# A pause on GpSimd that waits for SyncE's answer, and one-hots made by a scalar for each edge

## The chip, the cores and the metric

The kernel runs on one core of one Trainium2 chip. The metric is the device time of one execution in microseconds (us); lower is better. The engines are named as the profile names them: PE is TensorE, DVE is VectorE, ACT is ScalarE, POOL is GpSimd and SP is SyncE, which here only issues DMAs and waits.

## The reference, cut to what matters

A graph network of three layers over 6250 nodes with 256 features and 100000 edges, sorted by the node that they end in:

```python
ew = edge_attr @ edge_w + edge_b                       # 100000 x 256, the same in each layer
for l in range(3):
    residual = x
    msg = relu(x[src] * ew)                            # the gather of 100000 rows
    for i in range(3):                                 # by edge type
        h = segment_sum(msg * (edge_type == i), dst)   # 6250 x 256
        out += (h / max(count_i, 1)) @ weights[l, i]
    out += x @ roots[l] + biases[l]
    x = residual + relu(out)
return layernorm(x0 + x)
```

## The kernel before, in words

The edges are cut into 391 pairs; a pair is 2 x 128 edges, and two pairs share one row buffer (a quad, `xs`, 128 x 2 x 2 x 256). The 391 pairs of a layer are walked in one hand-written order, one loop step `it` for each; a step takes up several pairs at different stages:

- `gather` (nine pairs ahead): `gather_pair` issues two indirect DMAs from POOL's queue (L900), each of which fetches 128 rows of 1 KB by the indices in `src_i`, and behind them zeroes a tile `breath` of 128 x 256 that nothing reads (L904). The first six pairs of a layer are gathered in the layer before (`gather_early`). Eight quads of row buffers rotate.
- `make_ew` (PE, L602 and L606): the weights of the edges, into PSUM.
- `weigh` (about three pairs ahead): DVE multiplies the gathered rows by them (L627), ACT takes the relu (L629).
- `one_hot` (two pairs ahead, once for a quad): DVE compares the numbers 0 to 119 with the place of each edge, for four columns of 128 edges at once (L634, 128 x 480). In layer 0 it also adds the two one-hots of a pair into one bf16 tile (L638), for counting.
- `reduce` (PE, L644): four fp32 matmuls sum the pair's rows by the one-hots into `h_p`; in layer 0 a bf16 matmul against ones counts the edges (L647).
- `add` (DVE, L659): adds `h_p` into an accumulator `acc`, at a place read from a register.

Every few pairs a block of 128 nodes is finished (`node_mul`, `node_end`): PE multiplies `acc` by the layer's weights (L687), DVE scales and adds (L718, L721), and SP writes the block to `x_mid` (L723), from which the next layer gathers. In the last layer the block is normalised instead (L738) and written out (L740). SP also loads the edge attributes (`load_at`, L560), 147 times in all, and the weights.

Each engine works through its instructions in the order in which they are written here (`tc.manual_schedule()`); waits between engines are put in from the tiles that they share. At the start of layer 0, twelve comparisons with a scalar for each partition (`find_came`, L568) stand in DVE's order.

Of the kernel before, what the change touches and what calls it, by code (L numbers as in the profile page):

```python
# [8 lines left out]
F32 = mybir.dt.float32  # L9
BF = mybir.dt.bfloat16  # L10
I32 = mybir.dt.int32
AF = mybir.ActivationFunctionType
ALU = mybir.AluOpType
# [429 lines left out]
def ordered_path(ctx, tc, x, attr_laid, A, weights, roots, biases, edge_w, edge_b, out, src, src_i, seg, place_i, consts, x_root,  # L443
# [6 lines left out]
    nc = tc.nc  # L450
    P = 128
# [8 lines left out]
    DC = D // P  # L460
    WK = R * WIN
# [10 lines left out]
    ident, ones, iota_w = consts  # L472
# [3 lines left out]
    x_mid = [dram.tile([N, D], F32, name=f"x_mid{l}") for l in range(L - 1)]  # L476

    big = ctx.enter_context(tc.tile_pool(name="big", bufs=1))
# [26 lines left out]

    acc = big.tile([P, DC + 1, R, ASIDE + 2 * P + WIN], F32, name="acc")
    inv = big.tile([P, NT, R], F32, name="inv")
    breath = big.tile([P, 256], F32, name="breath")
    zero = big.tile([P, 1], F32, name="zero_o")
    nc.vector.memset(zero, 0.0)  # L510
    eps = big.tile([P, 1], F32, name="eps")
# [1 line left out]
    full_ones = big.tile([P, P], BF, name="full_ones")  # L513
# [15 lines left out]
    edge = ctx.enter_context(tc.tile_pool(name="edge", bufs=2))  # L529
# [7 lines left out]
    def first_of(p, n):  # L537
        return p == 0 or order[p - 1] // n != order[p] // n
# [31 lines left out]
    def layer(l, r_sb, b_sb, ats, early, pools):  # L570
# [5 lines left out]
        x_rows = x if l == 0 else x_mid[l - 1]  # L576
        w_sb = wpool.tile([P, R * DC, D], F32, name="w_sb")
        CH = DC + 1 if l == 0 else DC
        xs, ew_ps, ohs, h_ps, o_ps, rs = {}, {}, {}, {}, {}, {}
        x0s, mvs, oh_bs, t_ss, places = {}, {}, {}, {}, []  # L580
        r_next, ats_next, early_next = (None, None), {}, {}

        def gather(u):
            p = order.index(u)
            if p < FIRST:
                xs[u // 2] = early[u // 2]
            else:
                if first_of(p, 2):
                    xs[u // 2] = room(rows, D)
                gather_pair(nc, xs[u // 2], x_rows, src_i, u, breath)  # L590

        def pairs_of(q):
            return range(min(2, U - 2 * q))
# [15 lines left out]
        def gather_early(p):  # L609
            u = order[p]  # L610
            if first_of(p, 2):
                early_next[u // 2] = room(rows, D)
            gather_pair(nc, early_next[u // 2], x_mid[l], src_i, u, breath)

        def complete(q):
            for k in pairs_of(q):
# [14 lines left out]
        def one_hot(q):  # L631
            ohs[q] = edge.tile([P, 4, WK], F32, name="oh", bufs=3)
            n = 2 * len(pairs_of(q))
            nc.vector.tensor_tensor(ohs[q][:, :n, :], iota_w[:, None, :].to_broadcast([P, n, WK]),  # L634
                                    seg[:, 4 * q:4 * q + n, None].to_broadcast([P, n, WK]), op=ALU.is_equal)
            if l == 0:
                oh_bs[q] = edge.tile([P, 2, WK], BF, name="oh_b", bufs=3)
                nc.vector.tensor_tensor(oh_bs[q][:, :n // 2], ohs[q][:, 0:n:2], ohs[q][:, 1:n:2], op=ALU.add)  # L638

        def reduce(u):  # L640
            h_ps[u] = h_pool.tile([P, DC + 1, WK], F32, name="h_p")
            for d in range(DC):
                for i in range(2):
                    nc.tensor.matmul(h_ps[u][:, d, :], xs[u // 2][:, u % 2, i, d * P:(d + 1) * P],  # L644
                                     ohs[u // 2][:, u % 2 * 2 + i, :], start=(i == 0), stop=(i == 1))
            if l == 0:
                nc.tensor.matmul(h_ps[u][:, DC, :], full_ones, oh_bs[u // 2][:, u % 2, :], start=True, stop=True)  # L647

        def add(u):
            if places[:1] != [u // 8]:  # L650
# [109 lines left out]
        for it in range(-11, max(starts) + 7):  # L760
            def pair(k):
                return order[it + k] if 0 <= it + k < U else None
            if pair(AHEAD) is not None:
                gather(pair(AHEAD))
            if l < L - 1 and 0 <= it + AHEAD - U < FIRST:
                gather_early(it + AHEAD - U)
# [15 lines left out]
            if pair(0) is not None:  # L782
                reduce(pair(0))
# [39 lines left out]
            if pair(2) is not None and first_of(it + 2, 2):  # L823
                one_hot(pair(2) // 2)
# [68 lines left out]
def room(rows, D):  # L893

    return rows.tile([128, 2, 2, D], F32, name="xs", bufs=ROWS)


def gather_pair(nc, xs, x_rows, src_i, u, breath=None):
    for i in range(2):
        nc.gpsimd.indirect_dma_start(  # L900
            out=xs[:, u % 2, i, :], out_offset=None, in_=x_rows[:, :],
            in_offset=bass.IndirectOffsetOnAxis(ap=src_i[:, 2 * u + i:2 * u + i + 1], axis=0))
    if breath is not None:
        nc.gpsimd.memset(breath, 0.0)  # L904


@with_exitstack
def kernel(ctx, tc, x, src, dst, edge_attr, edge_type, weights, roots, biases, edge_w,
# [32 lines left out]
    with tc.tile_pool(name="look", bufs=1) as look, tc.tile_pool(name="look_p", bufs=2, space=PSUM) as look_p, \  # L941
# [17 lines left out]
        for u in schedule(N, E, 1)[0][:FIRST]:  # L959
            if u // 2 not in first_rows:  # L960
                j = 4 * len(first_rows)
                first_rows[u // 2] = x_root[:, j:j + 4, :].rearrange("p (k i) d -> p k i d", k=2)
            gather_pair(nc, first_rows[u // 2], x, src_i, u)
# [49 lines left out]
    with tc.If(unordered == 0):  # L1013
        ordered_path(tc, x, attr_laid, edge_attr.shape[1], weights, roots, biases, edge_w, edge_b, out, src, src_i, seg, place_i,
                     (ident, ones, iota_w), x_root, first_rows, node_i)
# [51 lines left out]
```

## Time and profile before

| | |
|---|---|
| time, median of 3 runs | 3261.3 us (3259.16 to 3263.47) |
| the profiled execution | 3254.66 us, its span 3252.8 us |
| busy: PE, DVE, ACT, POOL | 2544.4, 2047.7, 816.6, 2671.8 us |
| gathers on POOL (L900) | 2334 after the first 12 |
| zeroings on POOL (L904) | 1167 |
| mean granted clock of PE | 0.893 |

The span is the profiled execution as the engines saw it; its own time is 1.9 us longer. [...] "Issue" as a cause of idle time means that nothing that the profile shows was waited for.

### The profile page before, as it was taken

How to read it: one execution, taken by the hardware profiler on the slowest of the kernel's cores; microseconds unless marked ns; L12 is line 12 of the kernel's file. 1: busy time of each engine (PE TensorE's matmuls, PEld its weight loads, DVE VectorE, ACT ScalarE, POOL GpSimd, SP SyncE). 2: the span in 40 equal slices, each digit the busy share in tenths (PEclk: the TensorE clock that was granted, in tenths of full speed). 3: DMA queues.
4: the chain of work that ended last, by engine and by line, in shares of the span. 5: the costliest groups of instructions: out<-in, count | busy, mean ns of one | idle time of the engine just before them, and what ended most of it. 6: DMA issues, size and time to landing. Idle time of an engine off the chain costs nothing.

```text
span 3252.8 us, 53355 instructions
## 1 busy us (share of the span) xinstructions
PE 2544.4 (78%) x18484; PEld 2119.3 (65%) x18484; DVE 2047.7 (63%) x4306; ACT 816.6 (25%) x959; POOL 2671.8 (82%) x3522
## 2 busy tenths in 40 slices
PE   5888787888887778777878778777778777777776
PEld 4766666666666666666666666666666666666655
DVE  7766667777776555555555565455656666766754
ACT  2222222222222222222222222222222222222221
POOL 7888888888888788888888888878888888888886
PEclk9888989999998888889889898788888889999988
DMA  5444444334443334333334444434444444444433
GB/s 174 116 129 124 132 117 116 115 114 118 115 126 114 116 103 117 111 111 115 115 114 118 119 118 120 123 107 131 120 123 123 124 123 126 122 120 117 126 108 89
DMA packets 173312, 387.75 MB, mean 119 GB/s; under 512 B 43418, under 2 KB 78636, under 8 KB 173036
## 3 DMA queue, kind: packets, MB, share of 16 engines
q0 software_dynamic: 112608, 307.65, 33.4%
q1 hardware_dynamic: 53136, 68.50, 6.6%
q10 hardware_dynamic: 7292, 8.11, 0.8%
q8 instruction: 151, 2.47, 0.3%
q14 instruction: 125, 1.02, 0.1%
HBM read 364.62 MB, written 19.46 MB: 118 GB/s over the span
## 4 chain that ended last, share of the span: by engine, by line
POOL 63%; issue 14%; PE 12%; DMA 7%; DVE 3%; ACT 1%; POOLq 1%; DVEq 0%; ACTq 0%
POOL xs L900 54%; POOL breath L904 9%; PE h_p L644 5%; DMA xs<-x_mid,src_io 4%; PE o_p L687 3%; DMA xs<-in_x_dram,src_io 2%; PE ew_p L606 2%; DVE xs L627 1%; PE r_p L672 1%; PE ew_p L602 1%; POOLq L900 1%; DVE acc L659 0%; ACT xs L629 0%; DVE x_root L718 0%; ACT acc L704 0%
## 5 line engine op out<-in xcount | busy, mean ns | idle before, releaser
L900 POOL DMA_INDIRECT xs<-x_mid,src_io x1564 | 1520.1, 972 | 375.0 <-issue 357.9
L644 PE MATMUL h_p<-oh,xs 128*128 128x120 f32 x9336 | 1378.4, 300 | 283.8 <-DVE acc L659 212.1
L644 PEld LDWEIGHTS h_p<-oh,xs 128*128 128x128 f32 x9336 | 1279.8, 211 | 448.8 <-DVE acc L659 275.7
L627 DVE TENSOR_TENSOR xs<-ew_p,xs 128x512 f32<-128x512 f32 x1167 | 788.2, 687 | 998.1 <-DMA xs<-x_mid,src_io 689.4
L629 ACT ACTIVATE xs<-xs 128x1024 f32<-128x1024 f32 (+1 forms) x588 | 617.7, 1051 | 2360.3 <-DVE xs L627 2316.7
L900 POOL DMA_INDIRECT xs<-in_x_dram,src_io x770 | 757.5, 984 | 180.8 <-issue 176.4
L659 DVE TENSOR_TENSOR acc<-h_p,acc 128x240 f32 (+1 forms) x1173 | 519.4, 443 | 84.7 <-PE o_p L687 36.5
L687 PE MATMUL o_p<-w_sb,acc 128*128 128x256 f32 (+1 forms) x1716 | 487.9, 425 | 67.7 <-DVE x_root L718 34.6
L606 PEld LDWEIGHTS ew_p<-ew_sb,at 32*128 32x128 f32 x4692 | 287.8, 214 | 272.3 <-issue 265.3
L687 PEld LDWEIGHTS o_p<-w_sb,acc 128*128 128x128 f32 (+1 forms) x1716 | 340.7, 211 | 150.9 <-DVE acc L659 35.6
L602 PE MATMUL ew_p<-bias,full_ones 3*128 3x512 bf16 x1173 | 219.6, 407 | 270.4 <-DVE xs L627 255.1
L606 PE MATMUL ew_p<-ew_sb,at 32*128 32x256 f32 x4692 | 414.9, 448 | 3.9 <-issue 3.9
L904 POOL MEMSET breath<- 128x256 f32 x1167 | 384.9, 330 | 0.4
L634 DVE TENSOR_TENSOR oh<-iota_w,seg_o 128x480 f32<-128x480 f32 x588 | 381.8, 649 | 0.0
L672 PE MATMUL r_p<-r_sb,t_s 128*128 128x256 f32 x588 | 190.8, 455 | 60.4 <-ACT t_s L668 59.6
L718 DVE SCALAR_TENSOR_TENSOR x_root<-o_p,inv,x_root 128x256 f32<-128x256 f32 (+1 forms) x429 | 205.9, 480 | 32.2 <-PE o_p L687 25.1
L672 PEld LDWEIGHTS r_p<-r_sb,t_s 128*128 128x128 f32 x588 | 121.9, 230 | 82.8 <-ACT t_s L668 67.7
L704 ACT ACTIVATE acc<-zero_o 128x768 f32<-128x768 f32 (+1 forms) x150 | 140.3, 935 | 29.3 <-PE r_p L687 18.7
L602 PEld LDWEIGHTS <-full_ones 3*128 3x128 bf16 x1173 | 34.0, 91 | 120.2 <-issue 87.2
L647 PE MATMUL h_p<-oh_b,full_ones 128*128 128x120 bf16 x391 | 88.0, 225 | 0.0
L638 DVE TENSOR_TENSOR oh_b<-oh 128x240 bf16<-128x240 f32 x196 | 80.6, 411 | 6.7
L675 DVE TENSOR_TENSOR x_root<-r_p,b_sb 128x256 f32<-128x256 f32 x147 | 61.3, 417 | 10.5 <-PE r_p L672 8.9
(93 smaller groups left out, 554.8 us busy)
## 6 DMA issues: line engine op xcount, KB each, us to landing
at<-in_attr_laid_dram SPq DMA_DIRECT2D x147, 256.0 KB
xs<-x_mid,src_io POOLq DMA_INDIRECT x1564
xs<-in_x_dram,src_io POOLq DMA_INDIRECT x770
x_mid<-x_all SPq DMA_DIRECT2D x96, 128.0 KB
x_all<-in_x_dram ACTq DMA_DIRECT2D x8, 768.0 KB
x<-in_x_dram SPq DMA_DIRECT2D x48, 128.0 KB
out_dram<-x_all SPq DMA_DIRECT2D x48, 128.0 KB
w_sb<-in_L_gnn_weights_dram SPq DMA_DIRECT2D x3, 768.0 KB
```

Of the source, the lines that this page charges most:

```text
L602: nc.tensor.matmul(banks[j].rearrange("p i d -> p (i d)"), full_ones[j * A:j * A + PARTS, :], bias[j * A:j * A + PARTS].rearrange("p i d - ...
L606: nc.tensor.matmul(banks[j][:, i, :], ats[OCT * o // GROUP][j * A:(j + 1) * A, o % (GROUP // OCT), i, :], ew_sb[j * A:(j + 1) * A, :], sta ...
L627: nc.vector.tensor_mul(xs[q][:, k], ew_ps[2 * q + k], xs[q][:, k])
L629: nc.scalar.activation(there, there, AF.Relu)
L634: nc.vector.tensor_tensor(ohs[q][:, :n, :], iota_w[:, None, :].to_broadcast([P, n, WK]), seg[:, 4 * q:4 * q + n, None].to_broadcast([P, n, ...
L644: nc.tensor.matmul(h_ps[u][:, d, :], xs[u // 2][:, u % 2, i, d * P:(d + 1) * P], ohs[u // 2][:, u % 2 * 2 + i, :], start=(i == 0), stop=(i ...
L659: nc.vector.tensor_tensor(there, h_ps[u][:, :CH].rearrange("p c (r w) -> p c r w", r=R), there, op=ALU.add)
L672: nc.tensor.matmul(rs[c][:, 1, :], t_ss[c][:, d, :], r_sb[:, d, :], start=(d == 0), stop=(d == DC - 1))
L687: nc.tensor.matmul(o_p[:n, j, :], acc[:, d, r, slot:slot + n], w_sb[:, r * DC + d, :], start=(d == 0), stop=(d == DC - 1))
L718: nc.vector.scalar_tensor_tensor(root, o_p[:n, j, :], inv[:n, c, r:r + 1], root, op0=ALU.mult, op1=ALU.add)
L900: nc.gpsimd.indirect_dma_start(out=xs[:, u % 2, i, :], out_offset=None, in_=x_rows[:, :], in_offset=bass.IndirectOffsetOnAxis(ap=src_i[:, ...
L904: nc.gpsimd.memset(breath, 0.0)
```

## The change

`breath`, a tile of float32, becomes `echo`, of int32 and the same size. Behind each zeroing, SP is told to load a value of it whose bounds are 0 and 0. Since that value is known, the built program has no load: what is left on SP is one instruction that waits for POOL's zeroing and then counts up a semaphore of SP. The next pair's zeroing overwrites what SP would have read, so it waits for that count; on POOL this is an instruction of its own, which stands between the pair's second gather and its zeroing. There are 1167 answers in SP's order, among its 352 DMAs, and each stands where its gather stands in the loop.

The one-hots of a quad are made by four comparisons of 128 x 120, each with one scalar for each partition, in place of one of 128 x 480 between two tensors. In layer 0 the bf16 copy holds all four one-hots, not the two sums, and is made by ACT, not DVE; PE counts with two bf16 matmuls for each pair, not one.

```diff
-    breath = big.tile([P, 256], F32, name="breath")
+    echo = big.tile([P, 256], I32, name="echo")
...
-            nc.vector.tensor_tensor(ohs[q][:, :n, :], iota_w[:, None, :].to_broadcast([P, n, WK]),
-                                    seg[:, 4 * q:4 * q + n, None].to_broadcast([P, n, WK]), op=ALU.is_equal)
+            for t in range(n):
+                nc.vector.tensor_scalar(ohs[q][:, t, :], iota_w, seg[:, 4 * q + t:4 * q + t + 1], None,
+                                        op0=ALU.is_equal)
             if l == 0:
-                oh_bs[q] = edge.tile([P, 2, WK], BF, name="oh_b", bufs=3)
-                nc.vector.tensor_tensor(oh_bs[q][:, :n // 2], ohs[q][:, 0:n:2], ohs[q][:, 1:n:2], op=ALU.add)
+                oh_bs[q] = edge.tile([P, 4, WK], BF, name="oh_b", bufs=3)
+                nc.scalar.activation(oh_bs[q][:, :n], ohs[q][:, :n], AF.Copy)
 
         def reduce(u):
             h_ps[u] = h_pool.tile([P, DC + 1, WK], F32, name="h_p")
-            for d in range(DC):
+            for d in range(CH):
                 for i in range(2):
-                    nc.tensor.matmul(h_ps[u][:, d, :], xs[u // 2][:, u % 2, i, d * P:(d + 1) * P],
-                                     ohs[u // 2][:, u % 2 * 2 + i, :], start=(i == 0), stop=(i == 1))
-            if l == 0:
-                nc.tensor.matmul(h_ps[u][:, DC, :], full_ones, oh_bs[u // 2][:, u % 2, :], start=True, stop=True)
+                    nc.tensor.matmul(h_ps[u][:, d, :],
+                                     xs[u // 2][:, u % 2, i, d * P:(d + 1) * P] if d < DC else full_ones,
+                                     (ohs if d < DC else oh_bs)[u // 2][:, u % 2 * 2 + i, :],
+                                     start=(i == 0), stop=(i == 1))
...
-    if breath is not None:
-        nc.gpsimd.memset(breath, 0.0)
+    if echo is not None:
+        nc.gpsimd.memset(echo, 0)
+        nc.values_load_multi_w_load_instructions(echo[0:1, 0:1], engines=[mybir.EngineType.SP], min_val=0, max_val=0,
+                                                 skip_runtime_bounds_check_because="it is nought")
```

More of the change, by code (lines that the diff above doesn't have):

```diff
@@ L589, in gather @@
                     xs[u // 2] = room(rows, D)
-                gather_pair(nc, xs[u // 2], x_rows, src_i, u, breath)
+                gather_pair(nc, xs[u // 2], x_rows, src_i, u, echo)
         def pairs_of(q):
@@ L612, in gather_early @@
                 early_next[u // 2] = room(rows, D)
-            gather_pair(nc, early_next[u // 2], x_mid[l], src_i, u, breath)
+            gather_pair(nc, early_next[u // 2], x_mid[l], src_i, u, echo)
         def complete(q):
@@ L895, in room, with gather_pair @@
     return rows.tile([128, 2, 2, D], F32, name="xs", bufs=ROWS)
-def gather_pair(nc, xs, x_rows, src_i, u, breath=None):
+def gather_pair(nc, xs, x_rows, src_i, u, echo=None):
     for i in range(2):
```

## The prediction

> **What bounds the kernel now.** I read the page first: busy times, the chain that ended last, the costliest groups.
>
> ```profile
> span 3252.8 us, 53355 instructions
> ...
> PE 2544.4 (78%) x18484; PEld 2119.3 (65%) x18484; DVE 2047.7 (63%) x4306; ACT 816.6 (25%) x959; POOL 2671.8 (82%) x3522
> ...
> POOL 63%; issue 14%; PE 12%; DMA 7%; DVE 3%; ACT 1%; POOLq 1%; DVEq 0%; ACTq 0%
> ...
> L900 POOL DMA_INDIRECT xs<-x_mid,src_io x1564 | 1520.1, 972 | 375.0 <-issue 357.9
> ...
> L627 DVE TENSOR_TENSOR xs<-ew_p,xs 128x512 f32<-128x512 f32 x1167 | 788.2, 687 | 998.1 <-DMA xs<-x_mid,src_io 689.4
> L629 ACT ACTIVATE xs<-xs 128x1024 f32<-128x1024 f32 (+1 forms) x588 | 617.7, 1051 | 2360.3 <-DVE xs L627 2316.7
> L900 POOL DMA_INDIRECT xs<-in_x_dram,src_io x770 | 757.5, 984 | 180.8 <-issue 176.4
> ...
> L904 POOL MEMSET breath<- 128x256 f32 x1167 | 384.9, 330 | 0.4
> L634 DVE TENSOR_TENSOR oh<-iota_w,seg_o 128x480 f32<-128x480 f32 x588 | 381.8, 649 | 0.0
> ...
> L638 DVE TENSOR_TENSOR oh_b<-oh 128x240 bf16<-128x240 f32 x196 | 80.6, 411 | 6.7
> ```
>
> POOL sets the time. Its busy time and the idle time before the gathers, nearly all of it "issue", make 2671.8 + 375.0 + 180.8 = 3227.6 us of a span of 3252.8 us. DVE, by contrast, stands idle for 998.1 us in front of L627, mostly waiting for gathered rows. The timeline of POOL in layer 1 shows the beat:
>
> ```profile
> 1502.42 0.95 POOL L900 DMA_INDIRECT xs<-x_mid,src_io  x1 [0.17 <-issue]
> 1503.68 0.95 POOL L900 DMA_INDIRECT xs<-x_mid,src_io  x1 [0.31 <-issue]
> 1504.63 0.33 POOL L904 MEMSET breath<- 128x256 f32 x1
> 1505.12 0.95 POOL L900 DMA_INDIRECT xs<-x_mid,src_io  x1 [0.17 <-issue]
> ```
>
> A pair costs 1505.12 - 1502.42 = 2.70 us, and 1167 pairs make 3151 us. What changes the time must therefore change this beat: a longer gather, a longer pause, or a gap. So I looked at where the beat is broken.
>
> **Gathers that DVE lengthens.** By line, with shortest, middle and longest duration (ns):
>
> ```profile
> L900 POOL DMA_INDIRECT xs<-x_mid,src_io x1564: 942/952/1738, 1084.7 to 3233.6; - x196
> L900 POOL DMA_INDIRECT xs<-in_x_dram,src_io x770: 942/952/1435, 20.9 to 1083.1; - x193
> L900 POOLq EVENT_SEMAPHORE  x587: 17/43/43, 62.8 to 3226.9; - x196
> L904 POOL MEMSET breath<- x1167: 325/330/457, 23.3 to 3234.6; 128x256 f32 x195
> L904 POOLq EVENT_SEMAPHORE  x2: 43/604/1165, 14.9 to 16.2; - x2
> ```
>
> And from the timeline, a gather that is lengthened and, in the last line, the DVE instruction beside the first gather above:
>
> ```profile
> 1508.85 0.65 DVE L634 TENSOR_TENSOR oh<-iota_w,seg_o 128x480 f32<-128x480 f32 x1
> 1509.07 1.25 POOL L900 DMA_INDIRECT xs<-x_mid,src_io  x1 [0.30 <-issue]
> ...
> 1502.48 0.65 DVE L634 TENSOR_TENSOR oh<-iota_w,seg_o 128x480 f32<-128x480 f32 x1
> ```
>
> The middle gather takes 952 ns, the means are 972 and 984. The surplus is 1564 x 20 + 770 x 32 = 31.3 + 24.6 = 56 us. It comes from the one-hot. L634 at 1508.85, in front of the gather at 1509.07, makes that gather 1.25 us; L634 at 1502.48, just behind the gather at 1502.42, leaves it at 0.95. I matched all gathers in the trace with the DVE instruction running as they start: 244 exceed 948 ns by over 50 ns, 62 us together, and 219 of them (56 us) start inside an L634 or L638. Both read two SBUF tensors. The gather needs something at its start that they hold until they end.
>
> **The one-hots: what goes, what comes.** Both L634 and L638 leave DVE, so up to 56 us of longer gathers go with them: 0.095 us for each of 588 quads. In their place come 588 x 4 less 6 = 2346 comparisons with a scalar for each partition. The nearest row is L568, twelve such comparisons of 128 x 128 in a row:
>
> ```profile
> L956 DVE TENSOR_SCALAR limits<-limits x1: 556/556/556, 2.4 to 2.4; 1x782 f32<-1x782 f32 x1
> L957 DVE SCALAR_TENSOR_TENSOR limits<-limits x1: 962/962/962, 3.0 to 3.0; 1x782 f32<-1x782 f32 x1
> ...
> L568 DVE TENSOR_SCALAR came<-came,node_i x12: 273/284/755, 79.1 to 81.6; 128x128 f32<-128x128 int32 x12
> ...
> 79.11 2.79 DVE L568 TENSOR_SCALAR came<-came,node_i 128x128 f32<-128x128 int32 x12 [5.15 <-DMA came<-in_src_dram]
> 79.11 0.95 POOL L900 DMA_INDIRECT xs<-in_x_dram,src_io  x1 [0.17 <-issue]
> 80.37 1.02 POOL L900 DMA_INDIRECT xs<-in_x_dram,src_io  x1 [0.30 <-issue]
> 81.39 0.36 POOL L904 MEMSET breath<- 128x256 f32 x1
> 81.91 0.97 POOL L900 DMA_INDIRECT xs<-in_x_dram,src_io  x1 [0.16 <-issue]
> ```
>
> A comparison or limit of this kind runs faster for each column than an operation on tensors (L956 takes 556 ns where L957 takes 962 for the same 782 columns), and it collides with POOL both ways. Of the twelve some take the normal 280 ns and others up to 755, held until POOL's gather ends. POOL pays 1.02 - 0.95, 0.36 - 0.33 and 0.97 - 0.95, together 0.12 us, or 10 ns for each comparison. For 2346 of them that is 23 us. The ends: nothing, if they do not collide at that width (the gain is then the whole 56 us); twice the row, 47 us, since one stretch of 2.8 us is a small sample (the gain is then 9 us). I take the row.
>
> [...]
>
> DVE's own time: twelve comparisons in 2.79 us, with holds, are 0.23 us each, so 0.93 us for a quad against 0.65, 588 x 0.28 = 165 us more, less the 80.6 us of L638. It lies in the 998.1 us of idling before L627; without that cover it would cost 84 us.
>
> **The count in layer 0.** ACT takes over 196 copies of 128 x 480. At 1051 ns for 1024 columns that is at most as much each, 206 us, beside 2360.3 us of idle time. PE gets 391 more bf16 matmuls with their weight loads:
>
> ```profile
> L647 PEld LDWEIGHTS <-full_ones x391: 106/107/165, 37.4 to 1090.2; 128*128 128x128 bf16 x196
> L647 PE MATMUL h_p<-oh_b,full_ones x391: 216/216/308, 37.6 to 1090.3; 128*128 128x120 bf16 x196
> ...
> 24.00:1083.00 1059.00, 857.57 (x6439) 706.83 (x6439) 738.86 (x1526) 276.78 (x300) 878.87 (x1150) 0.90 0.42 123
> ```
>
> 391 x 0.216 = 84 us, on top of 857.57 us busy in the 1059 us of layer 0: 942, and still under 1059. POOL hides it, with a buffer of 16 pairs between. Cost on the path: 0. Without that cover it would be 84 us.
>
> **The wait for SP.** The zeroing of pair k now waits until SP has answered the zeroing of pair k-1. Between the two stand the two gathers of pair k, about 2.70 - 0.33 = 2.37 us of POOL's work. SP needs little for an answer: in the timeline its store followed DVE's result at once.
>
> ```profile
> 1508.19 0.43 DVE L721 SCALAR_TENSOR_TENSOR x_all<-x_root,x_all 128x256 f32<-128x256 f32 x1
> ...
> 1508.64 0.33 SPq L723 DMA_DIRECT2D x_mid<-x_all  x1
> ...
> L723 SPq DMA_DIRECT2D x_mid<-x_all x98: 245/320/330, 136.2 to 2178.8; - x98
> ```
>
> DVE ended at 1508.62, SP began at 1508.64. Two such hand-overs and a wait of 43 ns are about 0.1 us, against 2.37. Is the extra instruction in front of the zeroing paid by POOL? Its sequencer runs ahead: the waits ahead of the first zeroing are taken at 14.9 to 16.2 and that zeroing runs at 23.3. Matching the 587 waits at L900 with the gathers behind them, 579 were taken four instructions ahead. Behind the waiting instruction on POOL are the next pair's gathers; they are needed only after two gathers already in the queue. So 0.
>
> The other danger is SP's order: an answer can stand behind a DMA that waits for DVE or PE. I took each of SP's 352 DMAs at its time in this trace and the zeroing that, in the changed order, needs the answer behind it. For the 98 stores to `x_mid` the shortest margin is 7.0 us (the one at 2178.8), the middle one 15; for the loads it is 16.8 us and more, but for the first at the start, which is 0.9 us late. I count 1 us at the start, in the rounding.
>
> **The sum.** -56 + 23 + 0 + 0 = -33 us. The profiled execution took 3254.66 us, 6.6 us under the median of 3261.3; the difference is carried over as it is. Forecast: 3261.3 - 33 = 3228.3, so 3228 us, 1.0% faster. Its own range runs from no collision (3205) to 47 us of it (3252).
>
> **Rivals.**
> 1. No collision at all: the four comparisons run at the slower rate of L957, as their width or their scalar may have it, and touch nothing of POOL's. All 56 us are gained: 3205 us. For it: L738, below, takes 411 ns for 256 columns, no less than L638 for its 240. Against it: L568's holds.
> 2. Slower: the four comparisons follow each other so closely that POOL, once it waits, waits for all of them. One place in the trace shows it:
>
> ```profile
> L738 DVE TENSOR_SCALAR x_all<-x_all,mv x49: 411/416/939, 2301.4 to 3246.9; 128x256 f32<-128x256 f32 x48, 106x256 f32<-106x256 f32 x1
> ...
> 3107.79 0.41 DVE L738 TENSOR_SCALAR x_all<-x_all,mv 106x256 f32<-106x256 f32 x1
> 3107.85 1.74 POOL L900 DMA_INDIRECT xs<-x_mid,src_io  x1 [0.30 <-issue]
> 3108.11 0.65 DVE L634 TENSOR_TENSOR oh<-iota_w,seg_o 128x480 f32<-128x480 f32 x1
> ```
>
> The gather at 3107.85 took 1.74 us: it waited through L738 and the L634 behind it. A hold's price goes with its square (chance to hit, times mean rest). L634's 0.65 us cost 0.095 us a quad; a closed series of 0.93 us costs 0.095 x (0.93 / 0.65)^2 = 0.194 us, 114 us in all, a net +58: 3319 us. [...] It decides above 0.095 us of stall a quad. Against it: in L568 twelve in a row left POOL room. [...]
> 3. SP's answer is on the path: POOL's sequencer does not run ahead past the wait, and each zeroing starts a hand-over late. At 0.17 us, the shortest gap that POOL shows, 1167 x 0.17 = 198 us: 3460 us. Against it: the four instructions of lead.
> 4. What is lost equals what is gained (0.095 us a quad): no change.
>
> **How the numbers follow.** Forecast 0.60, rival 1 0.08, rival 4 (within 0.2%, 6.5 us, about what a measurement of this kernel can tell from no change) 0.08, rival 2 0.19, rival 3 0.05. Faster 0.68, same 0.08, slower 0.24. The range starts under rival 1, at 3200, and goes up to 3300, into the milder collisions of rival 2; what lies above is about 0.17.
>
> **What would show it.** Right: gathers' mean within 10 ns or so of their middle of 952; DVE's four one-hots with a middle near 280 ns and a tail up to some 700; gaps of POOL as before (0.17 and 0.30); no wait of the zeroing for SP; PE in layer 0 busy for less than 95% of it. Wrong: gathers or zeroings with a mean above 1000 or 400 ns (rival 2), idle time in front of L905 released by SP (rival 3).

## The result and the profile after

The changed kernel takes 3211.2 us (median of 4 runs, 3210.27 to 3213.65); the kernel before, run beside it, takes 3260.2 us (4 runs, 3258.21 to 3263.47). The ratio is 0.985, with an interval from 0.9833 to 0.9867: faster by 49 us, where 33 were predicted (3228). The profiled execution took 3213.65 us; against the 3254.66 us of the one before that is 41.0 us less, and these 41 us are what the two traces can account for.

The page of the changed kernel: span, busy times, the chain that ended last by engine, and groups.

```profile
span 3211.8 us, 58435 instructions
...
PE 2550.8 (79%) x18875; PEld 2120.9 (66%) x18875; DVE 2118.2 (66%) x5868; ACT 934.3 (29%) x1155; POOL 2627.7 (82%) x3522
...
POOL 58%; PE 19%; issue 12%; DMA 6%; DVE 3%; POOLq 1%; ACT 1%; SPq 0%; DVEq 0%; ACTq 0%
...
L901 POOL DMA_INDIRECT xs<-x_mid,src_io x1564 | 1493.3, 955 | 374.6 <-issue 237.6
...
L627 DVE TENSOR_TENSOR xs<-ew_p,xs 128x512 f32<-128x512 f32 x1167 | 766.1, 684 | 701.8 <-PE ew_p L606 346.2
...
L901 POOL DMA_INDIRECT xs<-in_x_dram,src_io x770 | 735.7, 956 | 180.9 <-issue 117.8
L606 PE MATMUL ew_p<-ew_sb,at 32*128 32x256 f32 x4692 | 429.1, 488 | 346.0 <-DMA at<-in_attr_laid_dram 342.0
...
L635 DVE TENSOR_SCALAR oh<-iota_w,seg_o 128x120 f32<-128x120 f32 x2346 | 569.7, 344 | 0.0
...
L905 POOL MEMSET echo<- 128x256 int32 x1167 | 389.5, 334 | 0.7 <-SPq L906 0.3
...
L639 ACT ACTIVATE oh_b<-oh 128x480 bf16<-128x480 f32 x196 | 117.8, 601 | 209.5 <-DVE oh L635 173.9
...
L645 PE MATMUL h_p<-oh_b,full_ones 128*128 128x120 bf16 x782 | 109.9, 224 | 0.0
```

The account of POOL closes. Its gathers were busy for 1520.1 + 757.5 = 2277.6 us and are now busy for 1493.3 + 735.7 = 2229.0: 48.6 less. The zeroings went from 384.9 to 389.5, 4.6 more. The idle time before the gathers was 375.0 + 180.8 and is 374.6 + 180.9: unchanged. What lies outside of POOL's busy time and these gaps was 25.2 us and is 3211.8 - 2627.7 - 374.6 - 180.9 = 28.6. Together, -48.6 + 4.6 + 3.4 and a further -0.4 from the gaps and POOL's other work make the -41.0 of the span.

By line, the same kernel, shortest, middle and longest duration in ns:

```profile
L901 POOL DMA_INDIRECT xs<-x_mid,src_io x1564: 942/952/1310, 1064.7 to 3189.3; - x196
L901 POOL DMA_INDIRECT xs<-in_x_dram,src_io x770: 942/952/1202, 20.7 to 1063.2; - x193
```

```profile
L905 POOLq EVENT_SEMAPHORE  x1168: 17/17/1213, 14.6 to 3188.0; - x195
L905 POOL MEMSET echo<- x1167: 312/330/473, 23.1 to 3190.3; 128x256 int32 x195
```

```profile
L635 DVE TENSOR_SCALAR oh<-iota_w,seg_o x2346: 249/278/818, 33.7 to 3194.2; 128x120 f32<-128x120 f32 x196
```

The middle gather is as long as before, 952 ns. What has gone is the tail: the longest went from 1738 to 1310, and the means from 972 and 984 to 955 and 956. The timeline shows a gather that starts inside the new comparisons:

```profile
1505.33 1.33 DVE L635 TENSOR_SCALAR oh<-iota_w,seg_o 128x120 f32<-128x120 f32 x4
1505.61 1.01 POOL L901 DMA_INDIRECT xs<-x_mid,src_io  x1 [0.30 <-issue]
...
1506.62 0.33 POOL L905 MEMSET echo<- 128x256 int32 x1
```

It starts at 1505.61, while the comparisons run from 1505.33 to 1506.66, and takes 1.01 us. In the trace of before a gather in the same position behind an L634 took 1.25.

Who waited for SP, and for whom SP waited (us in total, times, longest us), in two answers of the chain of waits, POOL's and SP's own queue:

```profile
POOL xs L901 <- issue: 355.3, 1167, 0.4
POOL xs L901 <- SPq L906: 180.1, 1095, 0.2
```

```profile
SPq L906 <- POOL echo L905: 2970.5, 1166, 4.8
...
SPq L724 <- DVE xs L627: 4.1, 15, 0.4
```

The answers cost POOL nothing here. The zeroing waited for one of them once, for 0.3 us (row L905 of the page). The 180.1 us that are now put down to SP are 1095 gaps of 0.16 us in front of gathers, the same gaps that were called "issue" before. SP for its part stands at the answers for 2970.5 us, in 1166 of 1167 cases: it is there first, and its stores to `x_mid` (L724) wait for DVE for at most 0.4 us.

### The profile page after: what moved, and what is told of

Read it like the earlier page. It is cut to its first block, busy times and chain, and to the rows that moved or that the text cites. A ratio compares the mean times of both kernels' runs of the same rounds, so it can differ in the third digit from the quotient of the medians.

```text
span 3211.8 us, 58435 instructions
## 1 busy us (share of the span) xinstructions
PE 2550.8 (79%) x18875; PEld 2120.9 (66%) x18875; DVE 2118.2 (66%) x5868; ACT 934.3 (29%) x1155; POOL 2627.7 (82%) x3522
## 4 chain that ended last, share of the span: by engine, by line
POOL 58%; PE 19%; issue 12%; DMA 6%; DVE 3%; POOLq 1%; ACT 1%; SPq 0%; DVEq 0%; ACTq 0%
POOL xs L901 49%; POOL echo L905 9%; PE h_p L645 9%; DMA at<-in_attr_laid_dram 5%; PE ew_p L606 4%; PE o_p L688 3%; PE r_p L673 2%; DVE xs L627 1%; POOLq L901 1%; DVE oh L635 0%; SPq L906 0%; POOLq L905 0%; DMA xs<-in_x_dram,src_io 0%; DVE acc L660 0%; DVE x_root L719 0%
## 5 line engine op out<-in xcount | busy, mean ns | idle before, releaser
L901 POOL DMA_INDIRECT xs<-x_mid,src_io x1564 | 1493.3, 955 | 374.6 <-issue 237.6
L627 DVE TENSOR_TENSOR xs<-ew_p,xs 128x512 f32<-128x512 f32 x1167 | 766.1, 684 | 701.8 <-PE ew_p L606 346.2
L901 POOL DMA_INDIRECT xs<-in_x_dram,src_io x770 | 735.7, 956 | 180.9 <-issue 117.8
L606 PE MATMUL ew_p<-ew_sb,at 32*128 32x256 f32 x4692 | 429.1, 488 | 346.0 <-DMA at<-in_attr_laid_dram 342.0
L606 PEld LDWEIGHTS ew_p<-ew_sb,at 32*128 32x128 f32 x4692 | 277.8, 232 | 508.9 <-DMA at<-in_attr_laid_dram 468.1
L635 DVE TENSOR_SCALAR oh<-iota_w,seg_o 128x120 f32<-128x120 f32 x2346 | 569.7, 344 | 0.0
L688 PE MATMUL o_p<-w_sb,acc 128*128 128x256 f32 (+1 forms) x1716 | 472.4, 415 | 27.5 <-DVE acc L660 14.1
L905 POOL MEMSET echo<- 128x256 int32 x1167 | 389.5, 334 | 0.7 <-SPq L906 0.3
L602 PE MATMUL ew_p<-bias,full_ones 3*128 3x512 bf16 x1173 | 175.5, 401 | 84.0 <-DVE xs L627 68.8
L639 ACT ACTIVATE oh_b<-oh 128x480 bf16<-128x480 f32 x196 | 117.8, 601 | 209.5 <-DVE oh L635 173.9
L645 PE MATMUL h_p<-oh_b,full_ones 128*128 128x120 bf16 x782 | 109.9, 224 | 0.0
L645 PEld LDWEIGHTS <-full_ones 128*128 128x128 bf16 x782 | 84.0, 107 | 3.4
```

What stands on the lines that cost most here:

```text
L602: nc.tensor.matmul(banks[j].rearrange("p i d -> p (i d)"), full_ones[j * A:j * A + PARTS, :], bias[j * A:j * A + PARTS].rearrange("p i d - ...
L606: nc.tensor.matmul(banks[j][:, i, :], ats[OCT * o // GROUP][j * A:(j + 1) * A, o % (GROUP // OCT), i, :], ew_sb[j * A:(j + 1) * A, :], sta ...
L627: nc.vector.tensor_mul(xs[q][:, k], ew_ps[2 * q + k], xs[q][:, k])
L635: nc.vector.tensor_scalar(ohs[q][:, t, :], iota_w, seg[:, 4 * q + t:4 * q + t + 1], None, op0=ALU.is_equal)
L688: nc.tensor.matmul(o_p[:n, j, :], acc[:, d, r, slot:slot + n], w_sb[:, r * DC + d, :], start=(d == 0), stop=(d == DC - 1))
L901: nc.gpsimd.indirect_dma_start(out=xs[:, u % 2, i, :], out_offset=None, in_=x_rows[:, :], in_offset=bass.IndirectOffsetOnAxis(ap=src_i[:, ...
```

## The experiments

Theory A: the gain is the time for which L634 and L638 held POOL's gathers; SP's answer and the count moved to ACT and PE bring nothing. Rival B: SP's answer makes the gain. Rival C: it comes from taking the count (L638) off DVE.

All twelve kernels ran on chips on which the kernel before takes not 3260 but 3681, 3630 and 3675 us (one chip for each group below). There POOL does not set the time, so that a ratio on them says little of what a part is worth at 3260 us, and theory A's forecasts of the time, made for 3260 us, missed. What their traces do show is how long gathers and zeroings are with each part, and what each part costs when POOL is not the last.

| kernel | median us | ratio to before, 95% interval |
|---|---|---|
| scalar one-hots alone (first chip of the three) | 3718.0 | 1.0092 [1.0075, 1.011] |
| SP's answer alone | 4168.1 | 1.131 [1.1288, 1.1333] |
| the count alone | 3686.9 | 1.0019 [1.0007, 1.0031] |
| the change without the answer | 3711.9 | 1.0081 [1.0065, 1.0097] |
| the whole change (second chip) | 4193.5 | 1.1555 [1.1532, 1.1577] |
| scalar one-hots alone | 3660.2 | 1.0083 [1.0069, 1.0096] |
| SP's answer alone | 4077.4 | 1.1253 [1.1227, 1.1279] |
| the change without zeroing and answer | 3690.1 | 1.0168 [1.0154, 1.0181] |
| before, light sums (third chip) | 3614.4 | 0.9839 [0.9825, 0.9852] |
| scalar one-hots alone, light sums | 3640.8 | 0.9909 [0.9896, 0.9922] |
| SP's answer alone, light sums | 3981.1 | 1.0855 [1.0827, 1.0882] |
| the whole change, light sums | 4074.0 | 1.1099 [1.1073, 1.1125] |

### The count alone, and what bounds the kernel on these chips

```diff
-                nc.vector.tensor_tensor(oh_bs[q][:, :n // 2], ohs[q][:, 0:n:2], ohs[q][:, 1:n:2], op=ALU.add)
+                nc.scalar.activation(oh_bs[q][:, :n], ohs[q][:, :n], AF.Copy)
...  (and the second counting matmul)
```

> The kernel before, with the bf16 copy on ACT and two counting matmuls for a pair alone. Theory A: 0.998 to 0.9995 (the collisions of L638, about 5 us, go; those of L634 stay); gathers' mean in layer 0 falls from 984 by 5 to 8 ns. Rival C: 0.985 to 0.99.

Measured: 0.19% slower. This kernel is also the nearest to the kernel before, so its page serves as the picture of these chips:

```profile
PE 65%; issue 13%; DVE 8%; another core or an unknown queue 8%; POOL 4%; DMA 2%; ACT 1%; DVEq 0%; POOLq 0%; ACTq 0%
...
L644 PE MATMUL h_p<-oh,xs 128*128 128x120 f32 x9336 | 1534.2, 316 | 689.0 <-DVE acc L659 361.9
L900 POOL DMA_INDIRECT xs<-x_mid,src_io x1564 | 1533.0, 980 | 638.2 <-issue 567.8
...
L900 POOL DMA_INDIRECT xs<-in_x_dram,src_io x770 | 752.7, 978 | 328.4 <-issue 290.0
```

PE stands for 65% of the chain and POOL for 4%, where POOL had 63% before. POOL's idle time in front of the gathers is 638.2 + 328.4 = 967 us, against 556. That fits a wait for free row buffers: by the DMA packets of POOL's queue (48 to a gather) a pair's rows have landed 27.8 us (middle) before DVE multiplies them, against 0.8 us in the trace of before. The durations of POOL's work are the same, 980 and 978 ns. Two rows of the page of before (the execution of 3254.66 us) to set beside it:

```profile
L644 PE MATMUL h_p<-oh,xs 128*128 128x120 f32 x9336 | 1378.4, 300 | 283.8 <-DVE acc L659 212.1
...
L606 PE MATMUL ew_p<-ew_sb,at 32*128 32x256 f32 x4692 | 414.9, 448 | 3.9 <-issue 3.9
```

PE's summing matmuls have a mean of 316 ns, against 300, and the mean granted clock is 0.834, against 0.893. More of the loss stands in idle time of PE. One row of PE's waits in the trace of before, and the same row in this one:

```profile
PE h_p L644 <- issue: 58.7, 82, 2.3
```

```profile
PE h_p L644 <- issue: 335.5, 318, 8.6
```

A stretch of its timeline shows both sides of it:

```profile
1507.94 1.15 PE L644 MATMUL h_p<-oh,xs 128*128 128x120 f32 x8
...
1508.93 0.78 PE L672 MATMUL r_p<-r_sb,t_s 128*128 128x256 f32 x2
...
1510.06 0.69 PE L672 MATMUL r_p<-r_sb,t_s 128*128 128x256 f32 x2 [0.35 <-issue]
1510.09 0.41 DVE L659 TENSOR_TENSOR acc<-h_p,acc 128x240 f32 x1 [2.48 <-PE h_p L644]
```

The sums end by the record at 1509.09, but the addition that needs them starts a whole microsecond later, at 1510.09, although DVE had been idle for 2.48 us; and PE's next matmuls pause for 0.35 us with nothing shown to wait for. From the recorded end of the sums to an addition in front of which DVE was idle, the middle time is 0.2 us in the trace of before, 0.04 in that of the changed kernel, and 0.9 here. The semaphores, the counters by which engines release each other, show on which side the lateness lies. PE counts up a semaphore when such work is done, and the record of the count stands 14 ns (middle) behind the recorded end of the matmul in the traces of before and of the changed kernel; here it stands 0.5 us behind, and over 2.7 us for a tenth of the counts. DVE's counts stand 11 ns behind their ends in all three. So PE is late in telling, or its matmuls end later than the profile, which models their ends, puts them; the trace does not say which. The page calls a wait "remote", or "another core or an unknown queue", when it ended with a count that stands far behind every recorded end; this kernel has no other core.

One thing weakens every "issue" on these pages: of POOL's 1172 counts 335 have a record here, of DVE's 4019 there are 2920, while the traces of before and of the changed kernel have 98% or more of them. A wait can be called "issue" because the record of what ended it is missing.

The middle gather takes 952 ns on these chips, too; with SP's answer alone, on the first of them, the middle zeroing takes 326 ns and the mean addition on DVE (L659) 446, against 330 and 443 in the trace of before. Why PE is held up there is open.

### Scalar one-hots alone

```diff
-            nc.vector.tensor_tensor(ohs[q][:, :n, :], iota_w[:, None, :].to_broadcast([P, n, WK]), ...
+            for t in range(n):
+                nc.vector.tensor_scalar(ohs[q][:, t, :], iota_w, seg[:, 4 * q + t:4 * q + t + 1], None,
+                                        op0=ALU.is_equal)
```

> The kernel before, with the four comparisons with a scalar alone (pause without an answer, bf16 sums on DVE as before). Theory A (the gain is that the one-hot no longer reads two SBUF tensors while a gather starts): 0.986 to 0.989 of the time before; the gathers' mean falls from 972 and 984 ns to 956 in layers 1 and 2 and to 960 to 968 in layer 0, where the bf16 sum (L638) still collides; the one-hots' middle is 278 ns with a tail to 800. Rival B (SP's answer made the gain): 1.00, means unchanged. Rival C (the counting moved off DVE made it): 1.00 or slower.

> The four comparisons alone again. Where POOL sets the time: theory A 0.986 to 0.989, gathers' mean 956 in layers 1 and 2, 960 to 968 in layer 0; rival B (SP's answer made the gain) 1.00. Where PE sets the time: 1.009 as in the run so far, for POOL's shorter gathers are worth nothing there.

Measured: 0.92% and 0.83% slower on two chips. The page of the first:

```profile
PE 2695.4 (73%) x18484; PEld 2244.0 (60%) x18484; DVE 2205.1 (59%) x6064; ACT 823.8 (22%) x959; POOL 2643.1 (71%) x3522
...
L901 POOL DMA_INDIRECT xs<-x_mid,src_io x1564 | 1500.7, 960 | 684.9 <-issue 578.3
...
L901 POOL DMA_INDIRECT xs<-in_x_dram,src_io x770 | 744.2, 966 | 349.5 <-issue 327.2
...
L905 POOL MEMSET breath<- 128x256 f32 x1167 | 387.6, 332 | 0.7
```

The gathers shorten as theory A says: means of 960 and 966 ns, against 980 and 978 with tensor one-hots on the same chip, with the zeroings at 332 against 329. That is 1564 x 20 + 770 x 12 = 40.5 us less of gathers and 3.3 us more of zeroing; the kernel is slower all the same, since POOL waits anyway. What is left to pay for, by exclusion, is DVE's time: 2205.1 us busy, against 2047.7 in the kernel before, 157 us, beside the 31 to 37 us by which the two runs are longer. No experiment shows that it is this.

### The change without the answer

```diff
-        nc.values_load_multi_w_load_instructions(echo[0:1, 0:1], engines=[mybir.EngineType.SP], ...
```

> The changed kernel with SP's answer taken away, the pause kept. Theory A: the same time as the changed kernel, 0.984 to 0.987 of the time before; no wait of PE for the attribute loads; the gathers' means 955 as in the changed kernel. Rival B: 1.00.

Measured: 0.81% slower, within the interval of the scalar one-hots alone (0.92%). Gathers' means are 959 and 958 ns. Moving L638 away as well brings the layer that reads `in_x_dram` from 966 to 958, 6 us in 770 gathers; in the trace of before, the 31 gathers that L638 held were 4.7 us longer together. Rival C has no more than that.

### SP's answer alone

```diff
+        nc.values_load_multi_w_load_instructions(echo[0:1, 0:1], engines=[mybir.EngineType.SP], ...
```

> The kernel before, with SP's answer alone. Theory A: 0.999 to 1.001; the gathers' means stay at 972 and 984; PE waits for late loads of the edge attributes for about 340 us (0 before), and that costs nothing. Rival B: 0.985 to 0.99. If the late loads cost time that the one-hots' gain hides in the changed kernel: 1.002 to 1.01.

> SP's answer alone again. Where POOL sets the time: theory A 0.999 to 1.001 and hardly a wait of the zeroing for SP, PE waiting some 340 us for late attribute loads; rival B 0.985 to 0.99. Where PE sets the time: 1.13.

Measured: 13.1% and 12.5% slower; the first expectation had 1% at most, the second, made after it, 13%. Of the first run, the rows of the zeroing, the sums and the additions on the page, then POOL's and SP's waits:

```profile
L644 PE MATMUL h_p<-oh,xs 128*128 128x120 f32 x9336 | 1619.2, 325 | 944.7 <-issue 591.5
...
L659 DVE TENSOR_TENSOR acc<-h_p,acc 128x240 f32 (+1 forms) x1173 | 522.7, 446 | 1152.1 <-remote 597.3
...
L904 POOL MEMSET echo<- 128x256 int32 x1167 | 382.4, 328 | 724.6 <-SPq L905 720.6
```

```profile
POOL echo L904 <- SPq L905: 720.6, 119, 11.2
```

```profile
SPq L723 <- DVE x_all L721: 721.0, 75, 16.7
```

The zeroing waits for SP for 720.6 us, in 119 waits of up to 11.2 us. SP in turn waits for DVE's results at its stores: for 721.0 us, 75 times, at the store to `x_mid` (L723) for L721, and besides at the store of the output (L740) in the last layer. (That the two sums are nearly equal is chance.) The answers stand in SP's order behind these stores. POOL runs ahead of DVE as far as its buffers let it, so here, where POOL is not the last, SP comes to a store long before its data; the answer behind it is late, and POOL stops before its zeroing.

How these stops become 480 us of time is not shown. They do not make the rows late: a pair's rows have still landed 25.6 us (middle) before DVE multiplies them, and 14 us or more for 99 of 100. Nor do they make the loads of attributes late, which SP issues 23 us (middle) ahead of their first use. What grows against the count alone is what was unexplained there: idle time of PE that is put down to "issue" (600.7 us in front of L644 by the view of PE's waits, against 335.5) and waits for late counts ("remote" in front of L659: 597.3 us, against 329.7), while the granted clock falls to 0.764. Gathers' means are 973 and 978 ns, against 980 and 978 in the count alone on the same chip: 11 us less, in a run 480 us longer, where scalar one-hots took 40. That speaks against rival B.

### The whole change, and the change without the pause

The second takes out zeroing and answer:

```diff
-        nc.gpsimd.memset(echo, 0)
-        nc.values_load_multi_w_load_instructions(echo[0:1, 0:1], engines=[mybir.EngineType.SP], ...
+        pass
```

> The changed kernel once more, beside its parts on one chip. Where POOL sets the time (a kernel before of about 3260 us): 0.983 to 0.987, as before. Where PE is held up and the kernel before takes about 3680 us, as in the four runs so far: the answers stand behind stores that wait for DVE, so POOL stops in front of its zeroing for some 700 us in all and the ratio is 1.10 to 1.14, as with the answer alone there.

> The changed kernel without the zeroing and without SP's answer. Where POOL sets the time: if the pause costs what POOL's beat says (0.33 + 0.17 in place of 0.30, 0.19 us a pair, 222 us), 0.91 to 0.93, unless PE or DVE, busy for 79% and 66% of the span, take over at 0.95 or so. If the pause gives something back that the beat does not show (comparisons that get no turn, transfers that collide): 0.97 to 1.02. Where PE sets the time: 1.00 to 1.01.

The changed kernel itself, 1.5% faster at first, is 15.6% slower on this chip, more than the 10 to 14% expected. Its gathers are as short as ever; POOL stops where it does with the answer alone:

```profile
L901 POOL DMA_INDIRECT xs<-x_mid,src_io x1564 | 1491.7, 954 | 495.7 <-issue 440.1
...
L901 POOL DMA_INDIRECT xs<-in_x_dram,src_io x770 | 734.2, 953 | 245.3 <-issue 210.8
L905 POOL MEMSET echo<- 128x256 int32 x1167 | 389.2, 333 | 776.6 <-SPq L906 771.4
```

Before the zeroing POOL stands for 776.6 us. Without zeroing and answer the kernel is 1.7% slower than before (at most 1% was expected), although POOL has 390 us less to do: once more, POOL is not the bound there. Why it is not as fast as the scalar one-hots alone (0.83% slower) is open.

### Light sums: is it the amount of PE's work?

To bring POOL back to the end of the chain, the last four kernels leave out of each pair's sums the second gather:

```diff
-                for i in range(2):
+                for i in range(1):
```

> The kernel before, with less work for PE: in reduce only the first of a pair's two gathers is summed (for i in range(1)); the second half of the edges is left out of the sums. That takes 2334 matmuls of about 0.275 us, some 640 us, from PE, so that POOL should set the time on whichever chip it runs. If it does: about 3230 to 3260 us, gathers' means 972 and 984, and POOL's gaps in front of the gathers 0.17 and 0.30. If the chips on which the kernel before takes 3630 to 3680 us are slow for another reason than PE, it stays above 3500.

> The kernel before with the light sums (only the first gather of a pair is summed) and the four scalar comparisons alone; the count in layer 0 stays on DVE, there is no answer from SP. Theory A (the gain is L634's hold on the gathers): the 50 us at L634 go, about 13 us of collisions come, so 37 us less than the light kernel before, 1.1%. Rival B (the answer made the gain): the same as the light kernel before, within 10 us.

> The kernel before with the light sums and SP's answer alone, tensor one-hots kept. Theory A: as the light kernel before, within 7 us, since the answer is there 2.3 us ahead of need as long as no store on SP's queue waits for DVE; gathers' means 972 and 984. Rival B: about 40 us less. If the stores' waits bite here too, it is slower, by up to some 400 us as with the whole sums, and the zeroing's idle time is put down to SP's queue.

> The changed kernel with the light sums (only the first gather of a pair is summed, in the count of layer 0 too). Theory A: the 37 us of the scalar comparisons and the 4 to 5 us that L638 held, about 42 to 49 us less than the light kernel before, 1.3 to 1.5%, and at most 10 us less than the light kernel with the scalar comparisons alone. Rival B: as the light kernel with the answer alone. Rival C (the count off DVE): the difference to the light kernel with scalar comparisons alone is over 20 us.

The premise failed: half of the summing matmuls gone brings 1.6%, not the 11% that lead to 3260 us. By the first expectation's own sign (above 3500 us) these chips are slow for another reason than the amount of PE's work. The page of the kernel before with light sums, and the matmul's shortest, middle and longest duration:

```profile
PE 47%; another core or an unknown queue 16%; issue 15%; DVE 14%; POOL 4%; DMA 2%; DVEq 1%; ACT 1%; POOLq 0%; ACTq 0%
...
L900 POOL DMA_INDIRECT xs<-x_mid,src_io x1564 | 1533.2, 980 | 592.6 <-issue 531.5
L644 PE MATMUL h_p<-oh,xs 128*128 128x120 f32 x4668 | 971.0, 348 | 902.1 <-DVE acc L659 502.1
...
L900 POOL DMA_INDIRECT xs<-in_x_dram,src_io x770 | 762.8, 991 | 284.5 <-issue 249.6
```

```profile
L644 PE MATMUL h_p<-oh,xs x4668: 262/275/569, 76.0 to 3593.7; 128*128 128x120 f32 x195
```

PE is still the largest part of the chain. With less to do it stands idle longer (902.1 us in front of L644, against 689.0 in the count alone), the granted clock falls to 0.747, and the mean matmul takes 348 ns where it took 316. A sum that starts at full clock takes 275 ns in the middle and one that starts while half of the clock is granted 421; 39% of them start so here (1827 of 4668), against 24% in the count alone. The busy time of the sums is 971.0 us, 204 more than half of the 1534.2 us of the count alone, so that work taken from PE is partly given back; how much of it by the lower clock, and what halves the clock, is not shown. The four do show the parts once more: against the light kernel before, scalar one-hots cost 26 us, the answer 367 and the whole change 460. So theory A's forecasts of the time failed with the premise; its forecast for the gathers is tested by the page of the scalar one-hots with light sums:

```profile
L901 POOL DMA_INDIRECT xs<-x_mid,src_io x1564 | 1501.5, 960 | 639.9 <-issue 574.0
...
L901 POOL DMA_INDIRECT xs<-in_x_dram,src_io x770 | 743.1, 965 | 316.4 <-issue 297.1
```

The gathers' means, 960 and 965 ns here, are 980 and 991 in the light kernel before: the shortening is there on the third chip, too.

## Why the prediction was right, and where it was not

**POOL sets the time: right.** 2627.7 + 374.6 + 180.9 = 3183.2 us of the span of 3211.8.

**The hold of L634 and L638: right, in place and size.** The prediction had 56 us of surplus over the middle gather; 1564 x 3 + 770 x 4 = 7.8 us are left. In the trace of before, 206 of the 243 gathers that exceed 948 ns by over 50 ns start strictly inside an L634 or L638, 55 us together (219 and 56 us by the prediction's matching), and the surplus of such a gather is what is left of the one-hot as it starts, less 0.13 us (middle). On all three chips of the experiments the gathers shorten with the scalar one-hots (954 to 960 ns and 953 to 966 in the six kernels that have them and a zeroing); with SP's answer alone they stay at 971 to 973 and 978 to 980. No experiment shows that this part alone brings the whole gain at 3260 us, since none ran where the kernel before takes that time; it rests on the account of POOL in the two traces.

**The new collisions: the term that was mis-sized.** Forecast +23 us, at 10 ns for a comparison, from the one stretch of L568. Even if all that is left were theirs, it is 7.8 us at the gathers and 4.6 at the zeroings, 12.4 us, or 5.3 ns each. (Matched as in the prediction, 68 gathers that start inside an L635 are 4.7 us longer together.) A stretch of 2.8 us was too small a sample, as the prediction feared. This is most of why the sum came out at -33 and the profile at -41. The further 8 us, from 41 to the medians' 49, lie in the choice of the profiled executions: the one before stands 5.6 us under its median, the one after 2.5 over. The prediction carried the first over to the result.

**Rival 2, a closed series that starves POOL: refuted.** It would show as gathers with a mean above 1000 ns and zeroings above 400; with scalar one-hots no kernel has a mean above 966 or 335. Comparisons and gathers are held in the trace of the changed kernel (up to 818 and 1310 ns, where the middle ones take 278 and 952); but the 114 us that the prediction estimated from the square of the series' length do not come, and the measured price is 5.3 ns a comparison at most. Rival 1, no collision at all, was nearer in its number (3205 us), but not in its mechanism: the comparisons of up to 818 ns are held ones. The 140 that take over 600 ns all end 0.04 to 0.11 us behind the end of a gather.

**DVE, ACT and PE: hidden, as argued, and one size was off.** DVE's busy time rose by 70.5 us (84 forecast), the four comparisons of a quad being busy for 0.97 us (0.93 forecast). ACT's copies took 117.8 us (206 at most). PE's second counting matmul was put at 84 us; the row of the counting matmuls on the two pages went from 88.0 us to 109.9, 22 more:

```profile
L647 PE MATMUL h_p<-oh_b,full_ones 128*128 128x120 bf16 x391 | 88.0, 225 | 0.0
```

The step took each matmul at its full duration, where matmuls overlap: 782 of 224 ns, one after the other, would be busy for 175 us, not 109.9. PE is busy for 877.63 us of the stretch from 20 to 1083 us, 83%, under the 95% that the prediction named. The cover that was named holds where POOL is last; on the other chips the kernels with scalar one-hots alone are 26 to 37 us slower.

**SP's answer: right on POOL, and two things missed behind it.** POOL did not wait (0.3 us, once). But each load of attributes now stands behind answers, too, and is asked for only when POOL has come that far. PE's wait in front of L606 went from 3.9 us to 346.0, 342.0 of it for `at`, and DVE's wait in front of L627, once for gathered rows, is now largely for PE. SP issues a load 2.9 us (middle) ahead of its first use, against 23.6 us before. In this trace it costs at most the 3.4 us that POOL's account leaves over. The prediction went through SP's DMAs as things that delay answers, and not the other way round.

**The danger that was named and set aside.** "An answer can stand behind a DMA that waits for DVE or PE": the margins of 7.0 us and more were taken from a trace in which POOL comes last, so that DVE is never far behind it. They are a property of that balance, not of the kernel. Where POOL runs ahead to the end of its buffers the margin is negative, and POOL stops for 595.6 to 776.6 us. The answer alone makes the kernel 12.5% to 13.1% slower there; by which path is open. Rival 3 had the wait in the wrong place, at each hand-over; it lies at stores. (Its 3460 us also leaves out the one-hots' gain; with the sum's -33 it would be 3426.)

## What to carry to other kernels

Match the gathers that are longer than the middle one with what VectorE runs as they start. Here 206 of the 243 longer ones started inside operations on two SBUF tensors, and the difference of mean and middle, times the count, 56 us, was what these took from GpSimd; a scalar for each partition in their place gave 44 us of it back, for 70.5 us of VectorE's busy time. A handshake between two engines puts one engine's order behind the other's: here what waited for a third engine in the answering queue became a wait of the first (720.6 us with the answer alone), and what stood behind the answers was asked for later (a load 2.9 us ahead of its first use, against 23.6). Take the margin of such a wait for the case that the engine runs ahead to the end of its buffers, not only from a trace in which it comes last.

## What was not expected of the hardware

The same kernel before took 3260 us beside the first result and 3630 to 3681 us on the three chips of the experiments, and on each of them its times agree to 0.6%. (The record does not name the chip of the first result.) The middle gather takes 952 ns on all. PE stands idle with no shown cause for longer (335.5 us in front of the sums, against 58.7), and its counts stand 0.5 us (middle) behind the recorded ends of its matmuls, against 14 ns. Taking half of the summing matmuls away gained 1.6%. What makes PE late there is not settled, nor why the answer makes it later, and so neither is which of the two times a reader's chip would show; the change is a gain of 1.5% for the one and a loss of 15.6% for the other.
